# Sorting W1's columns by W2's sign on chip, so that an edge is a maximum and a minimum

## The chip, the cores and the metric

The kernel runs on one core of a Trainium2 chip. The core has a matrix engine (PE, with its weight loads PEld), VectorE (DVE), ScalarE (ACT), GpSimd (POOL) and SyncE (SP), which work side by side, each through its own queue in order, and 16 DMA engines. The metric is the time of one execution in microseconds (us) on the device.

## The reference

The input is 32 entries of 512 nodes with 256 features and one 512 x 512 adjacency that is nearly empty. There are four graph layers. Layers 0 and 3 have this form, and the change is in them:

```python
pre_u = jnp.einsum('bud,dk->buk', h_t, W1[:d])
pre_v = jnp.einsum('bvd,dk->bvk', h_t, W1[d:])
hidden = jax.nn.relu(pre_u[:, :, None, :] + pre_v[:, None, :, :] + b1)
S = jax.nn.sigmoid(jnp.einsum('buvk,ko->buvo', hidden, W2)[..., 0] + b2[0])
a_t = jnp.einsum('buv,bud->bvd', S * A_a, h_t)
m_t = jnp.einsum('uv,bud->bvd', A_m, h_t) * h_t
z_t = beta1 * h_t + beta2 * (jnp.einsum('bvd,de->bve', a_t, Wa) + ba) + beta3 * (jnp.einsum('bvd,de->bve', m_t, Wm) + bm)
```

`S` is needed only where the adjacency isn't zero. For each such edge (u, v) and each entry the sum over 256 features of `W2 * relu(pre_u[u] + b1 + pre_v[v])` is wanted: the score of the edge. Layer 1 mixes the nodes with the adjacency, multiplies by a matrix, applies relu and adds its input. Layer 2 is an attention with a softmax over all 512 nodes.

## The kernel before

`Counts` counts the edges of every row. If the rows have too many, a branch (`excess > 0`) takes a dense path; with this input the sparse path runs, and everything below is in it.

**Edges as items.** `Edges.build` makes lists on chip. The 512 rows are four chunks of 128 partitions. Each chunk has eight items (`OWN`), and an item holds one edge for every row of its chunk; edges beyond eight go into four panels, whose rows may come from anywhere in a half. So there are 36 items (`ITEMS`), in the order `e.order`: chunks 0, 2, 1, 3, overlapping, the panels among the last eight.

**Groups.** The 32 entries are eight groups of four (`NB`). For each group and each of the layers 0 and 3, `pre` multiplies every chunk with W1 on PE, VectorE adds b1 (L596), ScalarE copies the other half (L597), and SP's queue writes both to a `table` in DRAM, with a row of 4 x 256 numbers for every node and side. For the self loops `pre` also adds the two halves (L599) and forms the weighted relu sum (L600) into `self_s`.

**The stream of edges** (`edges`) is 36 steps. A step fetches a tile `rows` (128 x 1024: 128 edges, four entries, 256 features) out of the table by an indirect DMA that GpSimd issues (L646), three steps ahead (`LEAD`; five in the two streams at the ends, which have more buffers and are called with `spare`). The side u of a chunk is loaded once on SP's queue as `mine` (L692). VectorE adds the two (L731). Then either VectorE takes relu and the weight over the whole tile (L739) and ScalarE sums the four entries one step later (`sums`, L717), or VectorE does both at once with an accumulation for each entry (L747). ScalarE gets every second item, and in the end streams all. After four items `exp_of` and `run_1` finish the sigmoid and multiply by the edge's value, and GpSimd writes each item into a sheet of cells in DRAM (`put`, L639). When all are in, `load` brings the sheet back as `SA` (L772).

**The middle stage** (`middle_one`) is the main work of PE, entry by entry: the products of layer 0 with `SA`, layer 1, the softmax of layer 2 (L958 on ScalarE to L964 on VectorE, whose result PE transposes at L1003), and `pre` of layer 3. `first` (loads, transposes at L578, copies at L579, `pre` of layer 0) and `last` (layer 3's output) run for neighbouring groups beside it.

**Order.** `weave` gives each piece a due time on a common scale in which a group's middle stage has length one, and so fixes the program's order; a scheduler then lays out each engine's queue. `edge_times` spreads the steps of a stream, `behind` keeps edge work from going ahead of the middle stage. `setup`, `setup_behind` and `setup_rest` build the lists and scale the other weights during the first group; they take temporary buffers from `big`.

Of the kernel before, what the change touches and what calls it, by code (L numbers as in the profile page):

```python
# [16 lines left out]
P = 128  # L17
# [17 lines left out]
EARLY = 20  # L35
CELLS = HALF * N
ITEMS = NC * OWN + 2 * PANELS
SPARE = NC // 2 * OWN * P + LINES
GROUP = NB * D
HELD = 12  # L40

# [7 lines left out]
class Model:  # L49


    def __init__(self, ctx, tc, a):
        nc = self.nc = tc.nc
        self.tc, self.a = tc, a
        const = self.const = ctx.enter_context(tc.tile_pool(name="const", bufs=1))
        self.ident = const.tile([P, P], F32, name="ident")
        make_identity(nc, self.ident)
        self.adj = const.tile([P, NC, N], F32, name="adj")
        for c in range(NC):
            nc.sync.dma_start(self.adj[:, c, :], a["adj"][c * P : (c + 1) * P, :])  # L60
        self.g0, self.g3 = self.gnn_first("L0_gnn"), self.gnn_first("L3_gnn")
# [36 lines left out]
    def gnn_first(self, L):  # L98
        nc, a, const = self.nc, self.a, self.const
        w = {"L": L}  # L100
        w["W1"] = self.load(f"{L}_W1", [P, 2 * DC, D], a[f"{L}_W1"].rearrange("(c p) k -> p c k", p=P))
        w["b1bc"] = self.bcast(f"{L}_b1", D)
        w["W2bc"] = const.tile([P, D], F32, name=f"{L}_W2bc")
        nc.scalar.dma_start(w["W2bc"], a[f"{L}_W2"].rearrange("k o -> (k o)").partition_broadcast(P))
        w["b2"] = self.bcast(f"{L}_b2", 1)
        w["nb2"] = const.tile([P, 1], F32, name=f"{L}_nb2")
        w["bcol"] = const.tile([P, DC, 1], F32, name=f"{L}_bcol")
        if L == "L3_gnn":
# [68 lines left out]
class Counts:  # L177
# [3 lines left out]
    def __init__(self, ctx, m):  # L181
# [4 lines left out]
        with tc.tile_pool(name="c_sb", bufs=2) as sb, tc.tile_pool(name="c_ps", bufs=1, space=PSUM) as ps:  # L186
            ones = sb.tile([P, N], F32, name="c_ones", bufs=1)
            nc.vector.memset(ones, 1.0)
            count = sb.tile([P, NC], F32, name="count", bufs=1)
# [17 lines left out]
            nc.vector.tensor_reduce(half, pc.rearrange("p (h c) -> p h c", h=2), AX.X, ALU.add)  # L207
            most = sb.tile([1, 1], F32, name="most")
            nc.vector.tensor_reduce(most, half, AX.X, ALU.max)
            nc.vector.tensor_scalar(self.excess, most, float(-LINES), None, ALU.add)  # L210
# [193 lines left out]
class Group:  # L404
# [3 lines left out]
    def __init__(self, sp, w, name):  # L408
# [7 lines left out]
        self.self_s = sp.grp.tile([P, NC, NB], F32, name=f"self_s{name[0]}")  # L416

# [5 lines left out]
class Sparse:  # L423
# [99 lines left out]
    def big(self, dtype, n, layer=None):  # L523

        self.bigs += 1
        if layer is None:
            layer = 3 if self.bigs <= NC else 0
        return self.act.tile([P, n], dtype, name="big", tag=f"SA{layer}", bufs=NC)

    def setup(self):  # L530


        for w in (self.m.g0, self.m.g3):
            self.nc.vector.tensor_scalar(w["nb2"], w["b2"], -1.0, None, ALU.mult)
        self.zero = self.act.tile([P, GROUP], F32, name="zero", tag="hWa3")
# [30 lines left out]
    def setup_rest(self):  # L566
        yield from self.rest

# [13 lines left out]
    def pre(self, g, b, hT):  # L582
# [3 lines left out]
        for c in range(NC):  # L586
            cs = slice(c * P, (c + 1) * P)
            if c % 2 == 0:
# [7 lines left out]
            nc.vector.tensor_tensor(puv[:, 0, :], pp[:, 0:D], w["b1bc"], ALU.add)  # L596
            nc.scalar.copy(puv[:, 1, :], pp[:, D:])  # L597
            both = self.small.tile([P, D], F32, name="both", bufs=1)
            nc.vector.tensor_tensor(both, pp[:, D:], puv[:, 0, :], ALU.add)  # L599
            nc.vector.scalar_tensor_tensor(  # L600
                both, both, 0.0, w["W2bc"], ALU.max, ALU.mult, accum_out=g.self_s[:, c, b : b + 1]
            )
# [47 lines left out]
    def edges(self, g, spare=(), own_tags=()):  # L650
# [12 lines left out]
        def own_1():  # L663
            self.sigmoid_of(own)
            diag = self.counts.diag.unsqueeze(2).to_broadcast([P, NC, NB])
            nc.vector.tensor_tensor(g.self_s, g.self_s, diag, ALU.mult)
            for q in range(2):
                diagonal = g.cells[q][q * HALF : q * HALF + HALF * (N + 1), :]
                diagonal = diagonal.rearrange("(c p a) b -> p c a b", p=P, a=N + 1)[:, :, 0, :]
                self.written(g, q, nc.sync.dma_start(diagonal, g.self_s[:, 2 * q : 2 * q + 2, :]))  # L670
# [9 lines left out]
        panels = [j for j in e.order if j >= NC * OWN][: len(own_tags)]  # L680

        def fetch(n):
# [4 lines left out]
            j = e.order[n]  # L687
            c = -j if -j in mine and j >= NC * OWN else j // OWN
# [13 lines left out]
            self.fetch(rows, g, e.iv[:, j : j + 1])  # L702
# [10 lines left out]
        def sums(k, rows):  # L713

            for b in range(NB):
                part = rows[:, b * D : (b + 1) * D]
                self.behind(nc.scalar.activation(part, part, AF.Identity, accum_out=g.s[:, k, b : b + 1]))  # L717
# [7 lines left out]
        todo = [(2, lambda: self.exp_of(w, own)), (4, own_1)]  # L725
        done = 0
        for k in range(ITEMS):
            for _ in range(2 if spare and len(ready) > 2 else 1):
                put()
            rows, other = fetched.pop(k)  # L730
            self.behind(nc.vector.tensor_tensor(rows, rows, other, ALU.add))  # L731
            if k + lead < ITEMS:
                fetch(k + lead)
            if summed:
                summed.pop(0)()
            if spare or k % 2 == 1 and k < ITEMS - 3:
                by_entry = rows.rearrange("p (b d) -> p b d", b=NB)
                w2 = w["W2bc"].unsqueeze(1).to_broadcast([P, NB, D])
                nc.vector.scalar_tensor_tensor(by_entry, by_entry, 0.0, w2, ALU.max, ALU.mult)  # L739
                summed.append(lambda k=k, rows=rows: sums(k, rows))  # L740
                if spare:
                    summed.pop(0)()
            else:
                for b in range(NB):
                    part = rows[:, b * D : (b + 1) * D]
                    at = g.s[:, k, b : b + 1]
                    nc.vector.scalar_tensor_tensor(part, part, 0.0, w["W2bc"], ALU.max, ALU.mult, accum_out=at)  # L747
            if k % 4 == 3 or k >= ITEMS - 3:
                ks = slice(done, k + 1)
                near = spare or k >= ITEMS - 5  # L750
                todo.append((k + (1 if near else 3), lambda ks=ks: self.exp_of(w, g.s[:, ks, :].rearrange(flat))))
                todo.append((k + (1 if near else 4), lambda ks=ks: run_1(ks)))
                done = k + 1
            while todo and todo[0][0] <= k:
# [695 lines left out]
```

## Time and profile before

Three runs took 2977.59 us in the median (2975.59 to 2987.02). One execution was profiled.

| | us |
|---|---|
| profiled execution, its own time | 2998.45 |
| its span | 2996.8 |
| POOL: 552 fetches into `rows` (L646) | 679.0 |
| POOL: 576 writes into the cells (L639) | 697.6 |
| DVE: 552 additions of 1024 (L731) | 666.4 |
| DVE: 272 relu and weight over 1024 (L739) | 329.4 |
| DVE: 1120 with accumulation over 256 (L747) | 414.0 |
| DVE: `pre`, 256 each of L596, L599, L600 | 104.9, 107.3, 107.3 |
| ACT: 1088 sums over 256 (L717) | 439.6 |

These are sums of durations over the span, one group of instructions a row; 24 of the 576 fetches and additions go by the name `rows_more` and are not in them. A group's time says what an engine does, not what the kernel waits for: several engines are busy at the same time. Two other views are used for that. One lists, for each engine, whom it waited for, with the total in us, the number of times and the longest. The other gives each engine's busy time in chosen stretches of the span. The kernel moves 677.30 MB by DMA.

### The profile page before, as it was taken

To read this page: it belongs to the slowest core of one execution; us is meant where nothing else is said; L and a number is where in the kernel's file an instruction comes from. 1 tells how busy PE (TensorE), PEld (TensorE's weight loads), DVE (VectorE), ACT (ScalarE), POOL (GpSimd) and SP (SyncE) were. 2 spreads that over 40 slices of the span, in tenths; PEclk is the share of its full clock that TensorE was granted. 3 is DMA by queue.
4 is the path that set the end of the run, shared out by engine and by line. 5 is a ranking of instruction groups with operands and counts; after the bars stand their busy time and mean duration, and the time that the engine had idled before them with its cause. 6 is when DMAs were issued, how large, how long until landed. Compare 5 with 4: busy or idle time off the path is not lost. (4 is left out here: it accounts for less than half of the span.)

```text
span 2996.8 us, 32453 instructions
## 1 busy us (share of the span) xinstructions
PE 2690.0 (90%) x8645; PEld 1613.9 (54%) x8646; DVE 2307.1 (77%) x6035; ACT 1336.8 (45%) x4101; POOL 1555.3 (52%) x1328
## 2 busy tenths in 40 slices
PE   6367787989998999989999899989999899988998
PEld 3134344545664566546664466646565466644666
DVE  6874786889588885988778885888858896783494
ACT  3553454445344443544344443445434453453262
POOL 2662463646445673556536464466735564361183
PEclk9678998999999999999999999999999999999999
DMA  8875657796678867787677866687677866663474
GB/s 268 286 225 169 213 174 221 233 300 203 217 217 269 268 211 227 230 262 254 209 222 247 275 207 230 216 268 253 211 228 236 303 227 197 208 211 102 148 244 150
DMA packets 302143, 677.30 MB, mean 226 GB/s; under 512 B 52608, under 2 KB 170880, under 8 KB 293760
## 3 DMA queue, kind: packets, MB, share of 16 engines
q0 software_dynamic: 122688, 414.40, 42.9%
q1 hardware_dynamic: 160304, 223.52, 23.0%
q10 hardware_dynamic: 18960, 37.24, 3.4%
q8 instruction: 70, 1.15, 0.2%
q14 instruction: 121, 0.99, 0.1%
HBM read 529.02 MB, written 146.01 MB: 225 GB/s over the span
## 5 line engine op out<-in xcount | busy, mean ns | idle before, releaser
L646 POOL DMA_INDIRECT rows<-table,iv x552 | 679.0, 1230 | 795.5 <-DMA table<-puv 262.7
L639 POOL DMA_INDIRECT cells<-s,cell x576 | 697.6, 1211 | 420.6 <-DVE s L675 243.2
L731 DVE TENSOR_TENSOR rows<-rows,mine 128x1024 f32<-128x1024 f32 x552 | 666.4, 1215 | 101.4 <-DMA rows<-table,iv 72.8
L717 ACT ACTIVATE rows<-rows 128x256 f32<-128x256 f32 x1088 | 439.6, 406 | 445.4 <-DVE rows L739 396.6
L46 PE MATMUL pst<-adj,h 128*128 128x512 f32 x1024 | 452.2, 592 | 0.0
L747 DVE SCALAR_TENSOR_TENSOR rows<-rows,L_gnn_W2bc 128x256 f32<-128x256 f32 x1120 | 414.0, 417 | 1.6
L739 DVE SCALAR_TENSOR_TENSOR rows<-rows,L_gnn_W2bc 128x1024 f32<-128x1024 f32 x272 | 329.4, 1213 | 0.4
L46 PEld LDWEIGHTS pst<-adj,h 128*128 128x128 f32 x1024 | 192.8, 190 | 219.9 <-issue 217.6
L46 PE MATMUL pst<-L_gnn_Wa,hT 128*128 128x256 f32 x1024 | 248.8, 393 | 62.9 <-DMA hT<-xT 57.8
L46 PEld LDWEIGHTS pst<-L_gnn_Wa,hT 128*128 128x128 f32 x1024 | 198.9, 199 | 103.0 <-issue 59.2
L46 PE MATMUL pst<-eT,feats 128*128 128x512 f32 x512 | 237.7, 619 | 10.9 <-ACT eT L1004 10.9
L46 PE MATMUL pst<-adjT,zW 128*128 128x512 f32 x512 | 228.2, 599 | 11.6 <-ACT zW L916 9.7
L596 DVE TENSOR_TENSOR puv<-pst,bc_L_gnn_b 128x256 f32<-128x256 f32 x256 | 104.9, 416 | 162.4 <-DMA table<-puv 89.2
L597 ACT COPY puv<-pst 128x256 f32<-128x256 f32 x256 | 93.2, 371 | 288.1 <-DVE puv L596 225.9
L1061 PE MATMUL pst<-hWa,SA 128*128 128x256 f32 x896 | 220.3, 400 | 0.0
L1061 PEld LDWEIGHTS pst<-hWa,SA 128*128 128x128 f32 x896 | 213.8, 328 | 3.7 <-issue 1.7
L717 ACT ACTIVATION_READ_ACCUMULATOR rows<-rows 128x1 f32 x1088 | 204.7, 188 | 0.0
L860 ACT COPY flat<-SA 128x512 f32<-128x512 f32 x128 | 136.7, 1128 | 136.6 <-issue 62.9
L891 PE MATMUL pst<-flat,hWa 128*128 128x512 f32 x448 | 196.8, 592 | 0.0
L592 PE MATMUL pst<-w_L_gnn_W,hT 128*128 128x512 f32 x256 | 141.5, 681 | 53.9 <-ACT hT L579 36.5
L46 PEld LDWEIGHTS pst<-eT,feats 128*128 128x128 f32 x512 | 99.9, 198 | 133.2 <-issue 113.3
L46 PEld LDWEIGHTS pst<-adjT,zW 128*128 128x128 f32 x512 | 96.5, 191 | 133.4 <-issue 114.0
(176 smaller groups left out, 3984.2 us busy)
## 6 DMA issues: line engine op xcount, KB each, us to landing
table<-puv SPq DMA_DIRECT2D x256, 256.0 KB
SA<-cells POOLq DMA_DIRECT2D x64, 1024.0 KB
h<-in_x_dram SPq DMA_DIRECT2D x64, 512.0 KB
mine<-table SPq DMA_DIRECT2D x64, 512.0 KB
hT<-xT SPq DMA_DIRECT2D x36, 512.0 KB
xT<-hT ACTq DMA_DIRECT2D x32, 512.0 KB
x2T<-yT SPq DMA_DIRECT2D x32, 512.0 KB
x2s<-x ACTq DMA_DIRECT2D x64, 256.0 KB
```

Source lines behind the costliest of these rows:

```text
L46: nc.tensor.matmul(out, lhsT, rhs, start=(n == 0), stop=(n == len(pairs) - 1))
L592: nc.tensor.matmul(pp, hT[:, 0, ks], w["W1"][:, 0::DC, :], start=True, stop=False)
L596: nc.vector.tensor_tensor(puv[:, 0, :], pp[:, 0:D], w["b1bc"], ALU.add)
L639: ins = self.nc.gpsimd.indirect_dma_start(out=g.cells[half], out_offset=bass.IndirectOffsetOnAxis(ap=at, axis=0), in_=s, in_offset=None)
L646: self.nc.gpsimd.indirect_dma_start(out=rows, out_offset=None, in_=g.table, in_offset=bass.IndirectOffsetOnAxis(ap=at, axis=0))
L717: self.behind(nc.scalar.activation(part, part, AF.Identity, accum_out=g.s[:, k, b : b + 1]))
L731: self.behind(nc.vector.tensor_tensor(rows, rows, other, ALU.add))
L739: nc.vector.scalar_tensor_tensor(by_entry, by_entry, 0.0, w2, ALU.max, ALU.mult)
L747: nc.vector.scalar_tensor_tensor(part, part, 0.0, w["W2bc"], ALU.max, ALU.mult, accum_out=at)
L860: self.nc.scalar.copy(flat[:, r, :], SA[r][:, :, b])
L891: nc.tensor.matmul(pz, hWa[:, r, cs], flat[:, r, :], start=(r == 0), stop=False)
L1061: self.nc.tensor.matmul(pz[:, k * D : (k + 1) * D], SA[r][:, cs, b], hWa[:, r, :], start=(r + k == 0), stop=(alone and k == 1 and r == NC ...
```

## The change

**What is computed.** W2's weight `w` is pulled into W1 and b1. With U = w(pre_u + b1) and V = w pre_v, `w * relu(pre_u + b1 + pre_v)` is `max(U + V, 0) = max(V, -U) + U` where `w` is positive and `min(U + V, 0) = min(V, -U) + U` where it is negative. So the u side is stored as -U, a feature with a positive weight gives a maximum of the two rows, one with a negative weight a minimum, and the sum of the stored u side (`less`) is subtracted once for each edge. The features are therefore sorted: 112 (`SURE`) that must be positive, 112 that must be negative, and 32 in the middle (`MIXED`) that keep the old form. If W2 has fewer than 112 or more than 144 positive entries, the dense path is taken.

**What is new.** `ranks` finds each feature's place from W2 in `Counts`, ahead of the masks. `sorted_W1` builds two 0-or-weight matrices, transposes W1, multiplies, and writes the sorted W1, b1 and W2 over the old ones: for layer 0 at the head of `setup`, for layer 3 at the end of `setup_rest`.

**What is moved.** `pre` no longer computes the self loops; it takes the sum of the u side with the addition of b1. Each chunk's self loops become one more step of the stream, whose second operand SP's queue loads from the table; so a stream has 40 steps (`STEPS`), 36 items and four self steps, each after the first item of its chunk. A step is a maximum over 4 x 112, a minimum over 4 x 112, and an addition and a weighted relu over 4 x 32. A panel's u side differs from edge to edge, so there the u side is subtracted whole over 4 x 224. ScalarE sums three of four items and the self steps (`k % 4`, before `k % 2`); in the remaining ones one `tensor_reduce` sums all four entries. The `mine_more` panels are fetched at step 24 rather than 20.

```diff
-EARLY = 20
+EARLY = 24
 CELLS = HALF * N
 ITEMS = NC * OWN + 2 * PANELS
+STEPS = ITEMS + NC
 SPARE = NC // 2 * OWN * P + LINES
 GROUP = NB * D
 HELD = 12
+
+SURE = 112
+MIXED = D - 2 * SURE
+PLACE = {0: 0, 2: 1, 1: 2, 3: 3}
...
+        w["W2col"], w["b1col"] = (const.tile([P, DC, 1], F32, name=f"{L}_{n}col") for n in ("W2", "b1"))
+        nc.scalar.dma_start(w["W2col"], a[f"{L}_W2"].rearrange("(c p) o -> p c o", p=P))
         w["W1"] = self.load(f"{L}_W1", [P, 2 * DC, D], a[f"{L}_W1"].rearrange("(c p) k -> p c k", p=P))
-        w["b1bc"] = self.bcast(f"{L}_b1", D)
-        w["W2bc"] = const.tile([P, D], F32, name=f"{L}_W2bc")
-        nc.scalar.dma_start(w["W2bc"], a[f"{L}_W2"].rearrange("k o -> (k o)").partition_broadcast(P))
+        nc.scalar.dma_start(w["b1col"], a[f"{L}_b1"].rearrange("(c p o) -> p c o", p=P, o=1))
+        w["b1bc"] = const.tile([P, D], F32, name=f"{L}_b1bc")
+        w["W2bc"] = const.tile([P, MIXED], F32, name=f"{L}_W2bc")
...
+            signs = self.ranks(m, sb, ps, ones)
...
+    def ranks(self, m, sb, ps, ones):
...
+        pos, rank, far, place, sure = (sb.tile([P, DC, 2], F32, name=f"c_{n}", bufs=1) for n in ("p", "r", "f", "q", "s"))
+        nc.vector.tensor_scalar(pos, w2, 0.0, None, ALU.is_gt)
+        pb = ps.tile([P, DC, 2], F32, name="c_pb")
+        mm(nc, pb[:, 0, :], [(before, pos[:, 0, :])])
+        mm(nc, pb[:, 1, :], [(before, pos[:, 1, :]), (ones[:, 0:P], pos[:, 0, :])])
+        pn = ps.tile([1, 2], F32, name="c_pn")
+        mm(nc, pn, [(ones[:, 0:1], pos[:, c, :]) for c in range(DC)])
...
+        nc.vector.tensor_scalar(rank, pos, -1.0, 1.0, ALU.mult, ALU.add)
+        nc.vector.tensor_tensor(rank, rank, turned.to_broadcast([P, DC, 2]), ALU.mult)
+        nc.vector.tensor_tensor(rank, rank, pb, ALU.add)
+        nc.vector.tensor_scalar(far, rank, float(SURE), float(SURE), ALU.is_ge, ALU.mult)
+        nc.vector.tensor_tensor(place, rank, far, ALU.add)
+        nc.vector.tensor_scalar(far, rank, float(D - SURE), float(SURE - D), ALU.is_ge, ALU.mult)
+        nc.vector.tensor_tensor(place, place, far, ALU.add)
+        nc.vector.tensor_scalar(sure, place, float(2 * SURE), None, ALU.is_lt)
...
+        self.sorted_W1(self.m.g0)
...
+        self.sorted_W1(self.m.g3)
+        yield
+
+    def sorted_W1(self, w):
+
+        nc = self.nc
+        t = self.big(F32, 2048, 0)
+        W1T = t[:, 0 : 2 * N].rearrange("p (c d) -> p c d", c=DC)
+        by_v, by_u = (t[:, k * N : (k + 1) * N].rearrange("p (c d) -> p c d", c=DC) for k in (2, 3))
+        for to, scale in ((by_u, w["su"]), (by_v, w["sv"])):
+            for c in range(DC):
+                nc.vector.tensor_scalar(
+                    to[:, c, :], self.m.upto_D, w["place"][:, c, :], scale[:, c, :], ALU.is_equal, ALU.mult
+                )
+        for c in range(DC):
+            pt = self.psum()
+            for r in range(2 * DC):
+                nc.tensor.transpose(pt[:, r * P : (r + 1) * P], w["W1"][:, r, c * P : (c + 1) * P], self.m.ident)
+            nc.scalar.copy(W1T[:, c, :], pt)
+        for k, to in enumerate((by_u, by_v)):
+            pp = self.psum()
+            for d in range(DC):
+                rs = slice((DC * k + d) * P, (DC * k + d + 1) * P)
+                mm(nc, pp[:, d * D : (d + 1) * D], [(W1T[:, c, rs], to[:, c, :]) for c in range(DC)])
+            nc.scalar.copy(w["W1"][:, DC * k : DC * (k + 1), :], by_two(pp))
+        pp = self.psum()
+        for k, (col, to) in enumerate(((w["b1col"], by_u), (w["W2col"], by_v))):
+            mm(
+                nc,
+                pp[:, k * D : (k + 1) * D],
+                [(col[:, c, :].to_broadcast([P, P]), to[:, c, :]) for c in range(DC)],
+            )
+        nc.vector.tensor_copy(w["b1bc"], pp[:, 0:D])
+        nc.vector.tensor_copy(w["W2bc"], pp[:, D + 2 * SURE :])
...
-            nc.vector.tensor_tensor(puv[:, 0, :], pp[:, 0:D], w["b1bc"], ALU.add)
+            sure = slice(0, 2 * SURE)
+            less = g.less[:, PLACE[c], b : b + 1]
+            nc.vector.scalar_tensor_tensor(
+                puv[:, 0, sure], pp[:, sure], 1.0, w["b1bc"][:, sure], ALU.mult, ALU.add, accum_out=less
+            )
+            nc.vector.tensor_tensor(puv[:, 0, 2 * SURE :], pp[:, 2 * SURE : D], w["b1bc"][:, 2 * SURE :], ALU.add)
             nc.scalar.copy(puv[:, 1, :], pp[:, D:])
-            both = self.small.tile([P, D], F32, name="both", bufs=1)
-            nc.vector.tensor_tensor(both, pp[:, D:], puv[:, 0, :], ALU.add)
-            nc.vector.scalar_tensor_tensor(
-                both, both, 0.0, w["W2bc"], ALU.max, ALU.mult, accum_out=g.self_s[:, c, b : b + 1]
-            )
...
+        def own_less():
+            self.behind(nc.vector.tensor_tensor(own, own, g.less.rearrange(flat), ALU.subtract))
+            self.exp_of(w, own)
...
+                one = g.less[:, a : a + 1, :].to_broadcast([P, len(k), NB])
+                self.behind(nc.vector.tensor_tensor(t, t, one, ALU.subtract))
...
+            if k < 0:
+                nc.sync.dma_start(rows, places[c, 1])
+            else:
+                self.fetch(rows, g, e.iv[:, j : j + 1])
...
+            rows, other = (t.rearrange("p (b d) -> p b d", b=NB) for t in fetched.pop(n))
+            ups, downs, mixed = (slice(0, SURE), slice(SURE, 2 * SURE), slice(2 * SURE, D))
+            self.behind(nc.vector.tensor_tensor(rows[:, :, ups], rows[:, :, ups], other[:, :, ups], ALU.max))
+            if n + lead < STEPS:
+                fetch(n + lead)
             if summed:
                 summed.pop(0)()
-            if spare or k % 2 == 1 and k < ITEMS - 3:
-                by_entry = rows.rearrange("p (b d) -> p b d", b=NB)
-                w2 = w["W2bc"].unsqueeze(1).to_broadcast([P, NB, D])
-                nc.vector.scalar_tensor_tensor(by_entry, by_entry, 0.0, w2, ALU.max, ALU.mult)
-                summed.append(lambda k=k, rows=rows: sums(k, rows))
+            nc.vector.tensor_tensor(rows[:, :, downs], rows[:, :, downs], other[:, :, downs], ALU.min)
+            nc.vector.tensor_tensor(rows[:, :, mixed], rows[:, :, mixed], other[:, :, mixed], ALU.add)
+            nc.vector.scalar_tensor_tensor(rows[:, :, mixed], rows[:, :, mixed], 0.0, w2, ALU.max, ALU.mult)
+            if k >= 0 and e.order[k] >= NC * OWN:
+                sure = slice(0, 2 * SURE)
+                nc.vector.tensor_tensor(rows[:, :, sure], rows[:, :, sure], other[:, :, sure], ALU.subtract)
+            to = g.s[:, k, :] if k >= 0 else g.self_s[:, PLACE[-1 - k], :]
+            if spare or k < 0 or k % 4 and k < ITEMS - 3:
+                line = rows.rearrange("p b d -> p (b d)")
+                summed.append(lambda to=to, line=line: sums(to, line))
                 if spare:
                     summed.pop(0)()
             else:
-                for b in range(NB):
-                    part = rows[:, b * D : (b + 1) * D]
-                    at = g.s[:, k, b : b + 1]
-                    nc.vector.scalar_tensor_tensor(part, part, 0.0, w["W2bc"], ALU.max, ALU.mult, accum_out=at)
-            if k % 4 == 3 or k >= ITEMS - 3:
+                nc.vector.tensor_reduce(to, rows, AX.X, ALU.add)
...
-    step = (b - a) / ITEMS
+    step = (b - a) / STEPS
```

## The prediction

> **What bounds the kernel now.** I read the engines' shares first, then the same shares by stretch, because an average over start, middle and end hides which of them can shrink.
>
> ```profile
> PE 2690.0 (90%) x8645; PEld 1613.9 (54%) x8646; DVE 2307.1 (77%) x6035; ACT 1336.8 (45%) x4101; POOL 1555.3 (52%) x1328
> ...
> 0.00:300.00 300.00, 180.01 (x507) 97.39 (x509) 202.45 (x503) 138.45 (x478) 134.32 (x130) 0.81 0.72 237
> 300.00:600.00 300.00, 250.41 (x737) 134.29 (x736) 235.12 (x627) 144.66 (x423) 158.98 (x138) 0.91 0.66 211
> 600.00:2600.00 2000.00, 1901.36 (x6225) 1148.08 (x6223) 1617.14 (x4390) 890.91 (x2656) 1090.74 (x917) 0.99 0.73 237
> ...
> 2834.00:2958.00 124.00, 112.40 (x383) 79.38 (x383) 111.00 (x145) 69.68 (x311) 91.93 (x71) 0.94 0.71 244
> ```
>
> The columns after the length of a stretch are the busy us of PE, PEld, DVE, ACT and POOL, then the granted clock, DMA share and GB/s. From 600 to 2600 PE is busy 95%: only 99 us of 2000 are idle. DVE follows with 81%. From 300 to 600 PE idles 50 us, before 300 it idles 120 us, and in the last round of edges (2834 to 2958) 12 us. The change gives PE nothing to save, so its gain is bounded by these idle stretches. What ends them is in the list of waits of PE, here for 600 to 2600 and 300 to 600:
>
> ```profile
> PE pst L1003 <- DVE ex L964: 29.6, 20, 3.3
> PE pst L592 <- ACT hT L579: 19.5, 5, 4.9
> PE pst L46 <- ACT zW L916: 8.3, 6, 3.2
> PE pst L934 <- DVE yT L923: 7.8, 8, 1.6
> ...
> PE pst L1003 <- DVE ex L964: 22.1, 7, 10.8
> PE pst L1003 <- DVE cols L963: 11.4, 2, 6.3
> ```
>
> (Total us, times, longest.) Adding up each whole list, DVE ends 60 us of PE's waits and ACT 33.5 us from 600 to 2600; from 300 to 600 it is 38 and 10.4. So 98 us wait for DVE and 44 for ACT. Last I read how the two engines meet:
>
> ```profile
> ACT rows L717 <- DVE rows L739: 396.6, 160, 12.2
> ```
>
> ScalarE stands 396.6 us in front of sums whose item VectorE hasn't finished, with its queue behind it.
>
> **Prices.** An instruction's duration overlaps the next one's start, so I price by start to start:
>
> ```profile
> 170.49 2.34 DVE L731 TENSOR_TENSOR rows_more<-rows_more,mine 128x1024 f32<-128x1024 f32 x2
> 172.76 2.35 DVE L739 SCALAR_TENSOR_TENSOR rows_more<-rows_more,L_gnn_W2bc 128x1024 f32<-128x1024 f32 x2
> 175.03 2.35 DVE L731 TENSOR_TENSOR rows<-rows,mine 128x1024 f32<-128x1024 f32 x2
> ...
> 1504.29 0.41 DVE L596 TENSOR_TENSOR puv<-pst,bc_L_gnn_b 128x256 f32<-128x256 f32 x1
> 1504.62 0.42 DVE L600 SCALAR_TENSOR_TENSOR both<-both,L_gnn_W2bc 128x256 f32<-128x256 f32 x1
> ```
>
> Four instructions of 1024 elements take 4.54 us, 1.135 each; one of 256 takes 0.335. That is 1.042 ns an element and 0.068 us an instruction. So 448 elements cost 0.535, 128 cost 0.201, 896 cost 1.001, 224 cost 0.301, 32 cost 0.101. A 256 with accumulation costs 0.345 (four of L747 start to end in 1.38). A ScalarE sum starts 0.40 after the last (97.71, 98.11, 98.50, 98.90), 1.6 an item. L739 already reads by entry and costs what the flat L731 does, so I price views with strides as flat; maximum and minimum as the addition.
>
> **The edge loop.** Before, an item that ScalarE sums costs VectorE 2 x 1.135 = 2.27, one that it sums itself 1.135 + 1.38 = 2.515. In the 14 ordinary streams that is 16 x 2.27 + 20 x 2.515 = 86.6 us. After, every step costs 0.535 + 0.535 + 0.201 + 0.201 = 1.472; a panel adds the 896 subtraction; an item kept on VectorE adds a reduction of 1024. No row shows one that long (the rows of TENSOR_REDUCE have 4 elements): below it is bounded by the one-source L131, 0.40 for 512, thus about 0.75; above by the four accumulations, 1.38. I take 1.135, as it reads what L731 reads. The stream is then 24 x 1.472 + 12 x 2.607 + 4 self steps x 1.472 + 4 x 1.001 + some 1.5 for a dozen small `less` subtractions = 78.0. Saved: 8.6 (with the bounds 5.6 to 13.2). The two streams at the ends sum everything on ScalarE: 81.7 before, 40 x 1.472 + 5.5 = 64.4 after, 17.3 saved.
>
> [...]
>
> **`pre`.** Two additions and an accumulation of 256 (1.015) become one accumulation over 224 and an addition of 32 (0.412): 0.60 saved 16 times a stream, 9.6 us, and PSUM is let go after one reader less. Over all: 14 x 8.6 + 2 x 17.3 + 16 x 9.6 = 309 us of VectorE's 2307, 77% to 67%.
>
> **ScalarE.** 12 more items in each ordinary stream and 4 in each end stream: 14 x 19.2 + 2 x 6.4 = 282 us, 45% to 54%. **DMA.** 64 self loads of 512 KB are 34 MB on 677; a share of 0.73 becomes 0.77. They go on SP's queue, where each waits for a `rows` buffer; behind it stand the `table<-puv` stores and the `hT` loads. The nearest row is `mine<-table` on the same queue, 146 us of waits in 22 cases for all streams: 64 more could stand 0 to 400 us, most of it not under PE. POOL's 1152 fetches and puts stay.
>
> **On the path.** *Start.* The ranks come ahead of the masks on VectorE and wait for two W2 loads of 4-byte elements; the branch at 12.1 us moves by 0 (the masks go first) to 8. Sorting L0's W1 ahead of the first `pre` (24.8 us) is 2.2 for transposes, 0.6, 3.4 for eight products at the cold 0.43, 0.6: 6.8, which may hide behind the load of `h` until 24. I take +6 in all, 0 to +14. L3's sorting falls where PE is idle. From 98 to 182 VectorE is busy without a gap: 25 items (25 x 0.80 = 20), ten `pre` (6), less four self steps (5.9), small ones and sorting (3.5) give 17 less; POOL is busy three quarters there and DMA 0.47 to 1.00, so I take half: -8, between -17 and 0. *Last round.* VectorE has 17 less to do, but PE itself idles 12 only: -6, between -12 and 0. *Middle.* If a wait in front of an engine goes as busy share to free share, DVE's 81% falls to 70%: 4.3 to 2.3, a cut by 46%. Of 98 us this is -45; -98 to 0. ACT's 45% rises to 55%: 0.82 to 1.22, half more of 44 us: +22; 0 to +70. The sum is 6 - 8 - 6 - 45 + 22 = -31. The profiled execution took 2998.45 us (span 2996.8), 21 above the median of the runs, 2977.59; taken off the median, that is 2947.
>
> **Rivals.** *ScalarE is tied to VectorE* (slower). Its queue is in order, and 396.6 us over 296 items (272 and 24 in `rows_more`) are 1.34 us of standing for each. With 14 x 28 + 2 x 40 = 472 at that price it stands 632 us, 236 more; with 1620 busy that is 75% of the span, and waits for `puv` come on top. If three in ten of those 236 us have a copy that PE needs behind them, PE loses 71; the sum is -31 - 22 + 71 = +18 on its own, and with SP's blocked self loads some +40: 2995 to 3018. It decides once VectorE falls an item behind where `hT`, `zW` or `eT` follow the sums. For it: the 12.2 us wait, and POOL's fetches already waiting 102 us for ACT. Against: an item is done in 1.47 rather than 2.27 us. *The waits are a chain of their own* (no change). L1003 waits for the softmax's chain, L958 to L964, some 4 us of dependent instructions; if this and not edge work ahead is the wait, only 9 of the 45 are won: 6 - 8 - 6 - 9 + 12 = -5, 2973. For it: waits of 1.5 us on average; against: the longest, 10.8. *All of it pays* (faster still): three quarters of DVE's waits go, -74 - 12 - 10 + 6 + 7 = -83, 2895; it needs ACT to stay out of the way. *It doesn't run at all:* with less than 112 or over 144 positive W2 entries the dense branch would take over; the seed's W2 has 133, so I give this under 1%.
>
> **How the numbers follow.** My forecast, near 2947 (its own range 2915 to 2963), has 0.43; all of it pays 0.13; no change 0.16; ScalarE tied 0.28. The range of 2890 to 3010 leaves out the far end of the first and of the last. Half a per cent is 15 us, about what this kernel's measurement can tell from no change: under 2963 is 0.43 + 0.13 = 0.56, within 0.16, above 2992 0.28.
>
> **What would show it.** Right: VectorE's busy time near 2000, ScalarE's near 1620; 600 to 2600 with PE idle less than 99 us, and L1003's waits for L964 halved; the first item's start (89.8) a little later, the last `pre` of the start earlier. Wrong: PE's waits for ACT over 80 us, or the wait of L717 for the last VectorE instruction of an item near 600; steps at 1.8 us; self loads holding up `table<-puv` on SP's queue.

## The result and the profile after

The changed kernel takes 3439.08 us in the median (3429.46 to 3453.77, four runs) where the kernel before, beside it, takes 2980.40: a ratio of 1.1541, with a 95% interval of 1.1492 to 1.1591. It is 459 us slower; the prediction was 2947. The profiled execution has a span of 3452.1 us, against 2996.8 before.

The first fence holds the shares of the engines on the page after and its row of the stretch from 600 to 2600 us (after the length: busy us of PE, PEld, DVE, ACT and POOL, the granted clock, DMA share and GB/s).

```profile
PE 2827.2 (82%) x8720; PEld 1688.9 (49%) x8720; DVE 2023.9 (59%) x5677; ACT 1610.4 (47%) x5517; POOL 1368.4 (40%) x1332
...
600.00:2600.00 2000.00, 1685.92 (x5202) 1007.48 (x5203) 1203.71 (x3302) 926.25 (x3157) 808.09 (x777) 0.93 0.65 210
```

VectorE has 283 us less to do, as wanted, and ScalarE 274 more. But PE now idles 314 of these 2000 us, 99 before, and the clock it is granted falls from 0.99 to 0.93. Over the whole span PE idles 625 us in place of 307, and is busy 137 us longer. The fullest engine, PE, is busy for 82% of it.

Next the costliest groups of the edge loop after: count, then busy us, mean ns of one, and the idle time just before them with what ended it. The second fence is the one addition of the kernel before.

```profile
L846 ACT ACTIVATE rows<-rows 128x256 f32<-128x256 f32 x1768 | 711.6, 405 | 459.3 <-DVE rows L862 278.1 <-DVE rows L869 80.2 <-issue 46.6
...
L736 POOL DMA_INDIRECT rows<-table,iv x548 | 577.3, 1054 | 1404.4 <-ACT rows L846 435.0 <-DMA table<-puv 264.7 <-DVE s L880 184.1
L867 DVE TENSOR_TENSOR rows<-rows,mine 128x448 f32<-128x448 f32 x608 | 375.3, 617 | 681.2 <-DMA rows<-table,iv 574.7 <-DMA mine<-table,iu 61.4 <-issue 20.4
L862 DVE TENSOR_TENSOR rows<-rows,mine 128x448 f32<-128x448 f32 x608 | 371.0, 616 | 214.4 <-DMA rows<-table,iv 178.1 <-DMA rows<-table 31.6 <-issue 4.7
...
L880 DVE TENSOR_REDUCE s<-rows 128x4 f32<-128x1024 f32 x168 | 201.5, 1202 | 0.7
```

```profile
L731 DVE TENSOR_TENSOR rows<-rows,mine 128x1024 f32<-128x1024 f32 x552 | 666.4, 1215 | 101.4 <-DMA rows<-table,iv 72.8
```

L862 is the maximum of a step and L867 the minimum that follows it in the program. Both need the fetched tile, and whichever comes first in VectorE's queue waits for it. If the queue kept the program's order, a step's L867 would never wait for that step's fetch. It waits 574.7 us, three times what L862 does; before, the one addition (L731) waited 72.8 us. So in most steps the minimum stands ahead of its maximum: in the order as built, in 441 of 640 (the count stated with the run e1 below). The trace doesn't name the steps, but in it the n-th minimum starts before the n-th maximum 473 times.

What stands behind such a wait is in the timeline of VectorE after (start, duration, line, and in brackets the idle time before), and under it PE's in the same stretch:

```profile
1224.44 0.29 DVE L869 SCALAR_TENSOR_TENSOR rows<-rows,L_gnn_W2bc 128x128 f32<-128x128 f32 x1
1231.63 0.62 DVE L867 TENSOR_TENSOR rows<-rows,mine 128x448 f32<-128x448 f32 x1 [6.89 <-DMA rows<-table,iv]
1232.17 0.28 DVE L868 TENSOR_TENSOR rows<-rows,mine 128x128 f32<-128x128 f32 x1
1232.49 0.29 DVE L869 SCALAR_TENSOR_TENSOR rows<-rows,L_gnn_W2bc 128x128 f32<-128x128 f32 x1
1232.70 0.68 DVE L1038 TENSOR_TENSOR hT<-hT,pst 128x512 f32<-128x512 f32 x1
1233.30 0.62 DVE L862 TENSOR_TENSOR rows<-rows,mine 128x448 f32<-128x448 f32 x1
...
1217.82 3.60 PE L1037 MATMUL pst<-mhT,L_gnn_Wm 128*128 128x512 f32 x8
1221.25 7.03 PE L51 MATMUL pst<-adj,h 128*128 128x512 f32 x16
1233.52 6.64 PE L1051 MATMUL pst<-WT,hT 128*128 128x256 f32 x16 [5.24 <-DVE hT L1038]
```

L1038 ends layer 0: it adds the products of L1037, which PE issued at 1217.82 and had done with 3.60 us later, by 1221.4. From 1224.73 VectorE has nothing to do, but at the head of its queue stands a minimum, and waits until 1231.63 for a transfer, with L1038 behind it. PE fills the time with L51 until 1228.28 and then waits 5.24 us. This is the view that explains the result: the wait is for an edge, the loss is in the middle stage.

In the list of PE's waits, 600 to 2600, it shows under the names of middle-stage work that stood behind edges:

```profile
PE pst L682 <- ACT hT L669: 83.2, 9, 13.0
PE pst L1051 <- DVE hT L1038: 73.4, 15, 6.0
PE pst L1142 <- DVE ex L1103: 38.0, 18, 5.0
```

Their old counterparts (L592 for L579, L912 for L899, L1003 for L964) had 19.5, 2.3 and 29.6 us in the same stretch; the prediction shows the first and the last, and this is the second:

```profile
PE pst L912 <- DVE hT L899: 2.3, 1, 2.3
```

### The profile page after: what moved, and what is told of

It is laid out like the page before. It is cut to its first block, busy times and chain, and to the rows that moved or that the text cites. A ratio compares the mean times of both kernels' runs of the same rounds, so it can differ in the third digit from the quotient of the medians.

```text
span 3452.1 us, 34150 instructions
## 1 busy us (share of the span) xinstructions
PE 2827.2 (82%) x8720; PEld 1688.9 (49%) x8720; DVE 2023.9 (59%) x5677; ACT 1610.4 (47%) x5517; POOL 1368.4 (40%) x1332
## 5 line engine op out<-in xcount | busy, mean ns | idle before, releaser
L736 POOL DMA_INDIRECT rows<-table,iv x548 | 577.3, 1054 | 1404.4 <-ACT rows L846 435.0
L846 ACT ACTIVATE rows<-rows 128x256 f32<-128x256 f32 x1768 | 711.6, 405 | 459.3 <-DVE rows L862 278.1
L867 DVE TENSOR_TENSOR rows<-rows,mine 128x448 f32<-128x448 f32 x608 | 375.3, 617 | 681.2 <-DMA rows<-table,iv 574.7
L729 POOL DMA_INDIRECT cells<-s,cell x576 | 622.7, 1081 | 319.5 <-issue 133.4
L862 DVE TENSOR_TENSOR rows<-rows,mine 128x448 f32<-128x448 f32 x608 | 371.0, 616 | 214.4 <-DMA rows<-table,iv 178.1
L51 PE MATMUL pst<-adj,h 128*128 128x512 f32 x1024 | 457.8, 598 | 8.8 <-ACT puv L692 8.6
L846 ACT ACTIVATION_READ_ACCUMULATOR rows<-rows 128x1 f32 x1768 | 334.1, 189 | 4.4 <-issue 4.4
L51 PEld LDWEIGHTS pst<-adj,h 128*128 128x128 f32 x1024 | 194.6, 192 | 233.2 <-issue 221.1
L51 PE MATMUL pst<-L_gnn_Wa,hT 128*128 128x256 f32 x1024 | 261.5, 408 | 55.2 <-DMA hT<-xT 45.9
L1051 PE MATMUL pst<-WT,hT 128*128 128x256 f32 x512 | 170.5, 505 | 119.6 <-DVE hT L1038 111.5
L51 PEld LDWEIGHTS pst<-L_gnn_Wa,hT 128*128 128x128 f32 x1024 | 208.5, 208 | 99.0 <-issue 64.3
L51 PE MATMUL pst<-eT,feats 128*128 128x512 f32 x512 | 232.7, 608 | 27.1 <-ACT eT L1143 17.4
L51 PE MATMUL pst<-adjT,zW 128*128 128x512 f32 x512 | 225.6, 593 | 0.0
L1051 PEld LDWEIGHTS pst<-WT,hT 128*128 128x128 f32 x512 | 132.8, 265 | 166.8 <-DVE hT L1038 83.6
L880 DVE TENSOR_REDUCE s<-rows 128x4 f32<-128x1024 f32 x168 | 201.5, 1202 | 0.7
L1030 PE MATMUL pst<-flat,hWa 128*128 128x512 f32 x448 | 196.9, 592 | 0.1
L688 DVE SCALAR_TENSOR_TENSOR puv<-pst,L_gnn_b1bc 128x224 f32<-128x224 f32 x256 | 98.5, 385 | 140.8 <-PE pst L684 92.0
L869 DVE SCALAR_TENSOR_TENSOR rows<-rows,L_gnn_W2bc 128x128 f32<-128x128 f32 x610 | 175.4, 288 | 9.0
```

What stands on the lines that cost most here:

```text
L51: nc.tensor.matmul(out, lhsT, rhs, start=(n == 0), stop=(n == len(pairs) - 1))
L729: ins = self.nc.gpsimd.indirect_dma_start(out=g.cells[half], out_offset=bass.IndirectOffsetOnAxis(ap=at, axis=0), in_=s, in_offset=None)
L736: self.nc.gpsimd.indirect_dma_start(out=rows, out_offset=None, in_=g.table, in_offset=bass.IndirectOffsetOnAxis(ap=at, axis=0))
L862: self.behind(nc.vector.tensor_tensor(rows[:, :, ups], rows[:, :, ups], other[:, :, ups], ALU.max))
L867: nc.vector.tensor_tensor(rows[:, :, downs], rows[:, :, downs], other[:, :, downs], ALU.min)
L869: nc.vector.scalar_tensor_tensor(rows[:, :, mixed], rows[:, :, mixed], 0.0, w2, ALU.max, ALU.mult)
```

## The experiments

Two theories were set against each other. **The lost tie:** of a step's three first instructions only the maximum goes through `behind`; the minimum and the addition touch other columns, share no data with it, and so may be laid ahead of middle-stage work. **The ring:** ScalarE sums more, 64 more steps go through the same five `rows` tiles, so tiles come free late and fetches start late. Ratios are to the kernel before, run beside, with their 95% intervals.

### The tie

**e1_tied**, the changed kernel with

```diff
-            nc.vector.tensor_tensor(rows[:, :, downs], rows[:, :, downs], other[:, :, downs], ALU.min)
-            nc.vector.tensor_tensor(rows[:, :, mixed], rows[:, :, mixed], other[:, :, mixed], ALU.add)
+            self.behind(nc.vector.tensor_tensor(rows[:, :, downs], rows[:, :, downs], other[:, :, downs], ALU.min))
+            self.behind(nc.vector.tensor_tensor(rows[:, :, mixed], rows[:, :, mixed], other[:, :, mixed], ALU.add))
```

> Theory T (the lost tie): in the changed kernel only the maximum L862 is held behind the middle stage; the minimum L867 and the addition L868 share no data with it, so in VectorE's queue 441 of 640 steps have their minimum ahead of their maximum, among instructions of the middle stage, and there it waits for the fetch with the middle stage behind it. With both also held behind, all 640 steps start with the maximum; T expects VectorE's waits for rows to fall from 865 us to under 200 and the time from 3439 to 2910 to 3000. Theory R (ring: ScalarE sums three of four items, frees the five rows tiles late, so fetches are late): the tie changes nothing of that, 3300 to 3440, with POOL waiting over 350 us for L846.

Measured: 3121.46 us, 1.0434 (1.0386 to 1.0482). 318 of the 459 us are back, less than the theory expected; some 130 stay. Its waits of VectorE for fetches, and of POOL for a tile:

```profile
DVE rows L862 <- DMA rows<-table,iv: 159.5, 68, 13.2
...
POOL rows L736 <- ACT rows L846: 442.6, 128, 13.4
```

No minimum waits for a fetch any more, and 753 us have become 160. The second row is as large as in the changed kernel (435.0, in the kernel before 102.5): this the tie did not touch.

**e4_split** is the kernel before with nothing of the change but a cut, and **f3_split_tied** the same cut with both halves tied:

```diff
-            self.behind(nc.vector.tensor_tensor(rows, rows, other, ALU.add))
+            cut = GROUP // 2
+            self.behind(nc.vector.tensor_tensor(rows[:, :cut], rows[:, :cut], other[:, :cut], ALU.add))
...
+            nc.vector.tensor_tensor(rows[:, cut:], rows[:, cut:], other[:, cut:], ALU.add)
```

> The kernel before, with its addition L731 cut in two halves of 512 columns, the first held behind the middle stage as before, the second not. It adds 576 instructions of 0.068 us, 39 us of VectorE, and has nothing else of the change. Theory T expects the change's loss to appear in the old kernel: 3150 to 3450, with the second half waiting for rows several hundred us. Theory R expects 2980 to 3020.

> e4 (the kernel before with the addition of L731 cut into two halves) with the second half tied behind the middle stage too: the same instructions of the same lengths as e4 (3273). By the lost tie the loss goes: 2985 to 3015. If the finer cut costs by itself, by instructions or by the ring, it stays over 3100.

Measured: e4 3273.28, 1.0953 (1.0890 to 1.1016); f3 3004.90, 1.0085 (1.0055 to 1.0115). The waits of VectorE in e4, where L732 is the tied half and L737 the free one, and then in f3:

```profile
DVE rows L737 <- DMA rows<-table,iv: 334.4, 152, 11.1
DVE rows L732 <- DMA rows<-table,iv: 126.5, 45, 13.5
```

```profile
DVE rows L732 <- DMA rows<-table,iv: 94.6, 38, 12.6
```

The old kernel takes a tenth longer by one untied half, and nearly all of it comes back when the half is tied. The cut itself, 576 more instructions, costs 0.85% with both halves tied. This pair isolates the cause: same instructions, same lengths, another order.

**e2_half** (`k % 4` to `k % 2`: ScalarE's old share) and **e3_six** (six `rows` tiles), both untied:

> Only the share of ScalarE goes back from three of four items to every second. Theory R (late rows tiles through ScalarE's sums) expects most of the 460 us back: 3000 to 3150. Theory T (the lost tie) expects little, since 447 of 640 minima still stand ahead of their maxima: 3350 to 3480, VectorE's waits at L867 still over 450 us.

> A sixth rows tile, nothing else. Theory R expects the fetches to run a tile further ahead and 150 to 350 us back: 3100 to 3290. Theory T expects under 100 us: fetches are still issued in the same place of the program and minima still stand ahead: 3340 to 3440.

Measured: 1.1522 (1.1466 to 1.1578) and 1.1465 (1.1411 to 1.1519), against 1.1541. As long as the tie is missing, neither of the two is worth 1%, and both intervals overlap the changed kernel's.

### What stays when the tie is restored

All that follows starts from e1, but for f1, which starts from the kernel before. **e5_tied_half** has ScalarE's old share, **e6_tied_six** six tiles, **e7_tied_noless** leaves out the subtraction of `less`, **e8_tied_noself** the self steps, so neither of the two computes the whole result. Their expectations weigh three theories, A, S and L; e5's says what each one is. The edits of e5 and e6:

```diff
-            if spare or k < 0 or k % 4 and k < ITEMS - 3:
+            if spare or k < 0 or k % 2 and k < ITEMS - 3:
...
-pool("gath", 5)
+pool("gath", 6)
```

> On the kernel with the tie (3121 us), ScalarE sums every second item again. Theory A (what is left of the loss is ScalarE's in-order queue and the rows tiles that it frees late) expects 3000 to 3070, PE's waits for ACT from 106 us to under 85 and POOL's waits for L846 from 443 to under 280. Theory S (the four self steps and their loads) and theory L (the subtraction of less between ScalarE's sum and ScalarE's exp) expect 3100 to 3160: VectorE gets 4 us a stream more to do.

> On the kernel with the tie, a sixth rows tile. Theory A in its second half (late rows tiles) expects 3030 to 3090 and POOL's waits for L846 under 300 us. If only the order in ScalarE's queue matters, or S or L, it stays at 3105 to 3135.

> On the kernel with the tie, the subtraction of less from the sums is left out, for the items and for the self loops, so a sum goes from ScalarE to ScalarE's exp without VectorE between. The scores are then too large by the sum of the u side. Theory L expects 3010 to 3070, and ACT's waits in front of exp (L704, 137 us for L787 alone) to fall under 60. Theories A and S expect 3095 to 3125.

> On the kernel with the tie, the four self steps of a stream, their loads and the writes of the diagonal are left out, so the scores of the self loops stay zero; 36 steps, panels fetched at step 20. Theory S expects 2990 to 3060: a tenth of the steps, 64 loads on SP's queue and a fifth of ScalarE's added sums go. Theory A expects 3060 to 3100 by its share of the sums (64 of 176 added items), theory L 3100 to 3125.

Measured, against e1's 1.0434: e5 1.0188 (1.0151 to 1.0226), e6 1.0165 (1.0111 to 1.0219), e7 1.0328 (1.0276 to 1.0379), e8 1.0024 (0.9998 to 1.0050). POOL's wait for a last sum, 442.6 us in e1, is 199.4 in e5 and 280.8 in e6. With the tie back the ring does count: the same two edits that gave less than 1% before now give 2.5% and 2.7%. e8 lands in the range of its theory: without the self steps 4.1% are back. e7 lands between the ranges: the subtraction is worth 1.1%.

**e9_tied_half_six** has both, and **e10_lead4** also `LEAD = 4`:

> All three vector instructions of a step tied (e1, 3121), ScalarE sums every second item (as in e5, 3041) and six rows tiles (as in e6, 3041). If the two edits cure different waits (ScalarE's share frees a tile late; five tiles are few for 40 steps), they add up: 3121 - 80 - 80 = 2961, range 2950 to 2985, and POOL's wait of a fetch for the last sum falls under 150 us. If both cure the same wait (a fetch stands until ScalarE has let a tile go), the second finds little left: 3010 to 3040.

> e9 with fetches four steps ahead instead of three. If late fetches are still what VectorE stands for (DVE's waits for rows 130 to 160 us in e5 and e6), another 20 to 60 us go against e9. If the fetches are held by tiles that ScalarE has not let go, a longer lead finds no free tile and the time is that of e9 within 15 us, with more waiting on POOL.

Measured: 1.0054 (1.0035 to 1.0072) and 1.0051 (1.0026 to 1.0075). The two cures overlap: the second adds 1.1 to 1.3%, half of what it gives alone. With the longer lead VectorE waits less for fetches (54.6 us, 77.4 in e9), the time stays, and POOL doesn't wait more for a last sum (228.8 us, 240.4 in e9). So late fetches aren't what is left, and that the lead finds no free tile, as the second expectation had it, isn't shown. These are the best complete forms that were run; they don't beat the kernel before.

**f1_before_noself**, the kernel before without its self loops, and **f2_tied_noself_half_six**, e9 without the self steps, ask what VectorE's time is worth at all:

> The kernel before, with nothing of the change, but without the self loops: L599, L600, the sigmoid of the self loops and the writes of the diagonal are left out, 214 us of VectorE's 2307 and one reader less of PSUM for every chunk of pre. The middle term of the prediction (a cut of VectorE's busy share cuts PE's 98 us of waits for it) expects 2984 - 45 or more: 2900 to 2950. If the load of VectorE is not what PE's waits come from, it is within 20 us of the kernel before.

> e8 (no self loops at all, three instructions tied) with ScalarE summing every second item and six rows tiles: all three known costs of the ring taken away together. If the changed edge step can gain anything once these are gone, 2900 to 2960. If VectorE's time is not what bounds the middle stage, 2975 to 3000, as e8.

Measured: f1 2954.79, 0.9933 (0.9911 to 0.9956); f2 2901.05, 0.9754 (0.9728 to 0.9779). The rows from 600 to 2600 of f1, of f2 and of e9:

```profile
600.00:2600.00 2000.00, 1913.89 (x6261) 1159.46 (x6260) 1501.92 (x3826) 900.86 (x2671) 1104.31 (x926) 0.99 0.72 238
```

```profile
600.00:2600.00 2000.00, 1948.40 (x6412) 1180.37 (x6411) 1509.28 (x3932) 926.23 (x2762) 1034.47 (x964) 0.99 0.73 244
```

```profile
600.00:2600.00 2000.00, 1900.07 (x6221) 1150.58 (x6221) 1502.44 (x3996) 960.75 (x3013) 1016.15 (x915) 0.98 0.76 248
```

The third number is PE's busy time: 1901 in the kernel before, 1914, 1948 and 1900. VectorE's is the same in all three, some 1505, against 1617 before. So VectorE's load alone doesn't decide: with equal load PE's idle time is 86, 52 and 100 us. f1 gains 23 us from 184 us less of VectorE, just above the 20 us that its rival allowed. The 45 us of its expectation were for a fall to 70%; in this stretch f1's fall is to 75%, for which the prediction's own rule gives an estimated 28 us (4.2 to 3.0, a cut by 29% of 98). PE's idle time there fell by 12.5, and the first product with `flat` comes at 225.8 us in place of 245.2, so much of the 23 can be the start's. f2 is 1.8% of the old time faster than f1, so the edge step itself can gain; but f2 also has six `rows` tiles and f1 five, and no run gave the kernel before a sixth.

The difference between e9 and f2, 3.0%, is the self loops alone, for which the old kernel paid 0.7%. Five runs looked for their cost. **e12_self_in_pre** and **e13_self_in_pre_half_six** put them back into `pre`, **g2_self_from_sbuf** is e13 with operands that don't hold PSUM, **g1_self_on_pool** is e9 with their loads on POOL's queue (first line), and **h1_self_on_vector** e9 with their sums on VectorE (second line):

```diff
-                nc.sync.dma_start(rows, places[c, 1])
+                nc.gpsimd.dma_start(rows, places[c, 1])
...
-            if spare or k < 0 or k % 2 and k < ITEMS - 3:
+            if spare or k >= 0 and k % 2 and k < ITEMS - 3:
```

In e12 and e13 `pre` gains this and a fourth instruction, the weighted relu of the middle features, and the steps of the stream are 36; g2 reads `puv[:, 1]` in place of `pp[:, D:]` and writes to a bf16 scratch:

```diff
+            for s, op, to in ((ups, ALU.max, at[0]), (downs, ALU.min, at[1])):
+                v = pp[:, D + s.start : D + s.stop]
+                nc.vector.scalar_tensor_tensor(pp[:, s], v, 1.0, puv[:, 0, s], ALU.mult, op, accum_out=to)
+            nc.vector.tensor_tensor(pp[:, mixed], pp[:, D + 2 * SURE :], puv[:, 0, mixed], ALU.add)
...
```

> e1 with the self loops back in pre: no self steps, no loads of theirs; a maximum, a minimum, an addition and a weighted relu with accumulations over 112, 112, 32 and 32 elements, read from PSUM (some 0.6 us, 256 times, 150 us of VectorE, where the self steps cost 94). Complete, unlike e8 (2994). If the self steps cost by their place in the ring of rows tiles, on SP's queue and on ScalarE, the time is near e8's: 2990 to 3030. If they cost by the work of VectorE, moving it does not help: 3070 to 3140.

> e12 with ScalarE summing every second item and six rows tiles: the ring with one tile more, 36 steps and ScalarE's old share. If the ring explains what e1 still loses, this is at or under the kernel before: 2930 to 2985. If VectorE's tie or its finer instructions cost something by themselves, it stays above: 2995 to 3030.

> e9 with one word changed: the loads of the self steps go through POOL's queue, where the fetches go, and no longer through SP's, where the puv stores and the loads of hT stand behind them. f2 (no self loops) is 0.030 of the kernel before faster than e9, some 90 us. If SP's queue is what the self steps cost, most of it comes back: 2920 to 2965. If they cost by their sums on ScalarE, their place in the ring and their transfers, nothing changes: 2990 to 3020.

> e13 (self loops in pre, half, six tiles; 1.0140) with the four self-loop instructions reading the copy that ScalarE makes into puv in place of PSUM, and writing to a small bf16 scratch, so that PE's buffer is let go after the same two readers as in f2. f2 has 0.9754, the old kernel pays 0.007 for its self loops. If the self loops in pre cost by holding PSUM, this comes to 0.980 to 0.993, under the kernel before: 2920 to 2960. If they cost by their instructions on VectorE in the middle of pre, 1.005 to 1.02: 2995 to 3040.

> e9 with the sums of the self steps on VectorE (one reduction of 1024, about 1.13 us) in place of ScalarE (four sums, 1.6 us): ScalarE some 100 us less, VectorE some 70 more. g1 and g2 have ruled out SP's queue and held PSUM. If ScalarE's added sums are what the self steps still cost, 2930 to 2975. If it is VectorE's work or the ring, as much or more than e9: 3000 to 3045.

Measured: e12 1.0323 (1.0286 to 1.0361), e13 1.0140 (1.0108 to 1.0173), g1 1.0094 (1.0060 to 1.0129), g2 1.0127 (1.0082 to 1.0172), h1 1.0069 (1.0043 to 1.0094). e12 gains 1.1% on e1 and still falls into the range of VectorE's work; the other four land on the side of no gain. So none of SP's queue, held PSUM and ScalarE's sums shows as the main cost of the self loops. Each move also brings work elsewhere: in g1 POOL waits 74.5 us for a tile in front of the loads, in h1 VectorE has 58 us more. What remains is the work on VectorE (the self steps add 83 us to f2's busy time, the form in `pre` 197 to 209), the finer order that it brings or, for the steps alone, their place among the `rows` tiles and their transfers, which e13 and g2 don't have. Which, no run tells, and it stays open.

## Why the prediction was wrong, point by point

**The prices were right.** A step was to cost 0.535 + 0.535 + 0.201 + 0.201; start to start the trace after shows 0.54 for L862 and L867, 0.20 for L868 and L869. Only where an L869 follows an L868 at once (259 times) is it mostly 0.32 between them, as from 1232.17 to 1232.49 above. The reduction of 1024, bounded between 0.75 and 1.38 and taken at 1.135, takes 1.13 from start to start (its row shows 1202 ns, with the overlap). VectorE's busy time was to be near 2000 and is 2023.9, ScalarE's near 1620 and is 1610.4. The 448 elements take 0.54 us from start to start, as the 0.068 us an instruction had it (616 ns is the duration of one, with the overlap).

**The start was right.** Six later and eight earlier were predicted. The first item starts at 94.0 us in place of 89.8, and the first product with `flat` (L891 before, L1030 after) comes at 244.2 in place of 245.2. But e1, with the same start but for the tie, has it at 249.1, so two us more or less can't be told here. The eight products of the sorting were priced at "the cold 0.43". That fits the trace before, where eight products of 128 (L578, at 21.26) take 1.74 us from start to start, 0.22 each, so an estimated 0.43 for 256, and 0.88 at 33.45; in the trace after they took 5.27 us (sixteen entries, from 20.86 to 26.13) in place of 3.4.

**The step that failed is the middle's**: "If a wait in front of an engine goes as busy share to free share, DVE's 81% falls to 70%: 4.3 to 2.3, a cut by 46%. Of 98 us this is -45." The share fell further, to 60% (also because these 2000 us now hold a sixth less of PE's instructions), and PE's idle time tripled; over the whole span PE's waits for VectorE went from 160 us to 354. From the first to the last product with `flat` it is 2951 us in place of 2519. The rule was the author's estimate, and takes an engine for a queue that serves whoever comes. But VectorE's queue ran in order (above, L1038 starts at 1232.70, after the minimum that waited 6.89 us), and its order is fixed when the kernel is built. What counts is which instruction stands at its head with a transfer still out. The prediction priced a step's four instructions by length and passed over the lines in the diff that say where they may stand: L731 was wholly inside `behind`, of its three successors only one is.

**The sizes.** By the ladder of ratios, 1.1541, 1.0434, 1.0054: the lost tie is 0.111 (some 320 to 330 us), ScalarE's share and the five tiles 0.038 (113 us), and 0.005 is left. That last 0.005 is two things: f2's gain of 0.025, and 0.030 for the self loops. The parts go by this order of the steps: taken out of e1 first, the self steps are worth 0.041 (e8).

**ScalarE's term (+22)** was of the right sign and too small: by e5 ScalarE's share is worth 0.025, some 73 us. It was sized by PE's waits for ScalarE; in the traces POOL's waits for a last sum grew most, 102.5 us before, 442.6 in e1. That the cost came by this wait fits e5 and e6, but isn't shown: e9 has more of it than e5 (240.4 and 199.4) and is faster.

**The self loads on SP's queue** were priced at up to 400 us "most of it not under PE". g1 moves them away and gains nothing, which fits. But the 64 self steps themselves, "4 self steps x 1.472" in a stream, are worth 90 us even in e9.

**The last round** was to shorten by 6. From the last product with `flat` to the end it is 256 us in place of 233, and e1 has 257 too: this part is not the tie's, and was not followed further. It stays in e9, which has 256 there: in the profiled executions e9's span is 20 us above the kernel before's, 7 of it at the start and 23 in the last round, while from the first to the last product with `flat` it is 10 shorter (2509 in place of 2519). So in these two executions what e9 lacks lies at the ends.

**The rivals.** "ScalarE is tied to VectorE" had the direction and two of its signs (PE's waits for ScalarE and POOL's for its sums grew), but not the place: L846 stands 358.3 us for VectorE (278.1 + 80.2), less than L717's 396.6, where 632 was worked out. None of the rivals named the order of VectorE's queue.

## What to carry to other kernels

When an instruction that carries an ordering tie is split, every piece needs the tie that is not reached through data by the piece that has it; otherwise the pieces are free to stand at the head of an in-order queue with their transfer still out (with one half free e4 took 1.0953 of the old time, with both tied f3 took 1.0085). In the profile this showed as a wait on the later piece of a step (L867's 574.7 us, L862's 178.1), where only the first can rightly wait. And a lighter engine shortens others' waits only if these were waits for its load (from 600 to 2600 the changed kernel has 413 us less for VectorE to do, f1 115; PE's idle time rose by 215 in the one and fell by 12.5 in the other): look at what the instruction ahead in its queue is waiting for before scaling any wait with a busy share.

## What the runs showed of the hardware

In these traces a longer wait in front of PE came with slower products behind it. The products of L912 before are L1051 after, the same 512; their groups in the two traces (mean ns of one, and idle before):

```profile
L912 PE MATMUL pst<-WT,hT 128*128 128x256 f32 x512 | 118.4, 383 | 8.5 <-DVE hT L899 8.2 <-issue 0.3
```

```profile
L1051 PE MATMUL pst<-WT,hT 128*128 128x256 f32 x512 | 170.5, 505 | 119.6 <-DVE hT L1038 111.5 <-issue 8.1
```

They waited 111 us longer and then ran 52 us longer. In the timeline above sixteen of them take 6.64 us after a wait of 5.24; on the chain that ended last in the kernel before sixteen take 3.69 (there after a wait of 2.10):

```profile
2708.19 3.69 PE pst L912 x16
```

So a wait of 5.24 us came to 8.2. The trace after shows what went with it, by the clock that PE was granted (the number before the last two) in three stretches, the first from the end of PE's last product:

```profile
1228.28:1232.68 4.40, 0.00 (x0) 0.00 (x0) 1.02 (x3) 0.00 (x0) 1.31 (x2) 1.00 0.89 250
1232.68:1239.51 6.83, 5.99 (x14) 4.85 (x15) 6.83 (x16) 2.20 (x9) 2.98 (x3) 0.50 0.68 255
1239.51:1246.00 6.49, 6.49 (x25) 5.21 (x25) 5.16 (x13) 2.59 (x11) 5.27 (x5) 1.00 0.45 126
```

It was 1.00 until 4.40 us after that end, then 0.50 for 6.83 us, 5.99 of them with products, and then 1.00 again. No run shows what sets it. What half the clock costs can be read from the trace before: four products of 128 x 512 (L592) take 3.58 us from start to start at 40.16, where the granted clock was 0.50, and 1.72 at 29.16, where it was 1.00.

The clock is also most of why PE's busy time grew by 137 us with only 75 more instructions than the 8645 before, which a sum of waits doesn't show. The granted clock is at half for 571 us of the trace after, with PE busy in 355 of them, and for 245 and 142 us of the one before. Of the 213 us more at half speed full speed would save half, an estimated 107.
